# A four-layer graph network: edge masks gathered in another layer, first blocks prepared before the table, four gather buffers, dense tiles kept off the end of the list, two row-end steps a tile

## Chip, cores and metric

The kernel runs on one core of a Trainium2 chip. The metric is the device time of one execution in microseconds. Before the change it is 3169.53 us, the median of three executions (3165.16 to 3173.18).

## What is computed

Four attention layers over one graph of N = 4096 nodes with C = 256 features. `adj` is a 4096 x 4096 matrix of 0 and 1 in int32; an edge is likelier among the low-numbered nodes, so the first rows have many edges and the last few. Every layer is followed by a residual sum and a LayerNorm. In short:

```
h = x @ W                                    # per layer
logit[i, j] = leaky_relu(f1[i] + f2[j])      # layer 0: 8 heads, + gate * sum_f Wc[f] * |curv[i,f] - curv[j,f]|
logit = where(adj > 0, logit, -big)          # layer 1: one head, no leaky_relu; layer 2: 4 heads
att = softmax(logit, over j);  out = att @ h # layer 2: elu(out) + x @ Wr + br, norm
x = layernorm(x + out)                       # layer 3: three such layers with elu (3.1, 3.2, 3.3), then the norm
```

## The kernel before

**Sparse work.** A tile has P = 128 partitions. Where the rows of a chunk or pair of chunks have few edges, the kernel does not go over all 4096 columns: it makes a list of the columns that have an edge, and fetches their rows of a table in HBM by an indirect DMA, which GpSimd issues. One such DMA fetches 128 rows and is called a gather here.

**Layer 0** (`layer0`, L770) goes by the 32 row chunks of 128 rows. Chunk 0 is dense (`rows0`, L448, all 32 column tiles, spread over the others by `next(dense)`). Chunks 1 to 31 go by their edges (`rows_by_edges`, L600): `EDGE_TILES[c]` tiles of 128 edges, 445 in all, in blocks of up to ten. A block has these steps:

- `middle` and `spread` (L626, L632) find which row every edge belongs to (VectorE, ScalarE and TensorE), and `nodes` (L641) makes from this the indices `idx` of the edges' nodes;
- `gather` (L656) fetches the rows of `table0`, one indirect DMA per tile (L659), into a buffer `g` of the pool `l0_got`, which has three;
- `differences`, `pair_terms`, `weights`, `values` (L662 to L689) make the attention weights and multiply the fetched rows by them. The first to read a gather is `d` (L666);
- `rows` and `add` (L691, L699) sum the rows by matmuls with a 0/1 matrix (L702). These matmuls are the last to read `g`, and free its buffer.

The loop at the end of the function calls these steps for blocks i to i + 4. The gather of block i + 2 is issued right after `values` of block i. The instructions of each engine run in the order that the tile scheduler has given them, which the source order and its own estimates decide; a queue does not overtake.

**Lists and masks.** Beside the blocks, `lane` (L1193) gives every tile a share of other work: `list_edges` (finds the columns of the next chunks' edges, almost all of it on VectorE, L905 to L922), `list_pairs` (the lists of columns for the pairs of chunks that the later layers use) and `job`. A pair q is 256 rows; of the 16 pairs, pair q has `PAIR_TILES[q]` tiles of 128 listed columns: 32, 25, 22, 20, 19, 18, 17, 16, 16, 15, 15, 14, 14, 14, 13, 13. For each listed tile of pairs 1 to 15 (251 tiles) a mask of 128 x 256 is needed. `listed_mask` (L1017) fetches it from the adjacency by an indirect DMA on GpSimd (L1020), converts it to bytes on VectorE (L1024), and SyncE writes it to `listed_d` in HBM. `LATE = 13` says which pairs' masks are made in layer 0: pairs 1 to 12, 211 tiles. The masks of pairs 13 to 15 (40 tiles) are put into `late_jobs` and made in layer 1 by `late_masks` (L1417). `mask_bytes` (L392, conversion at L402) makes byte masks for the pairs that are done densely. The job queue lets 7 masks be under way.

**Start of layer 0.** The first projection runs over 32 tiles; after every fourth, six steps of `list_edges` are taken. Then VectorE scales the 32 tiles of `V` (L1175), and SyncE writes each to `table0` (L1177). Only then does `rows_by_edges` open its pools, in memory that `V` and its neighbours have used, and make its constants: `number`, `place`, `count` (L707 to L712) and two memsets each for `dTs` (L619).

**Layers 1 to 3** go by pairs of chunks. `sequence` (L1252) sets the order of the tiles: the first `LEAD` dense tiles (`DENSE` says how many pairs are dense: 6 in layer 1, 1 in layer 2, 3 in each part of layer 3), then the listed tiles in order of the pairs, with the remaining dense tiles spread evenly among them. `attend` (L1266) runs over this order: for each tile the weights (VectorE, ScalarE) and, two tiles later, the products (TensorE: L1414, L1515 and L1519, L1605). After each tile it takes one step of `aside` and `rate` steps of the row ends, which norm the finished rows and project them for the next layer (L198, L209, L213). `rate` is 1.0 by default, 1.6 in layer 2. The gathers of these layers are at L1312. After the last tile the projection's sums set the next layer's scale, `V` is scaled, and the next table is written.

Of the kernel before, what the change touches and what calls it, by code (L numbers as in the profile page):

```python
# [54 lines left out]
I32 = mybir.dt.int32  # L55
# [19 lines left out]

LATE = 13
# [4 lines left out]
def gnn_stack(ctx: ExitStack, tc: tile.TileContext, a: dict, out: bass.AP):  # L81
# [366 lines left out]
    def rows0(chunks, ends, ps, ps_s, ps_acc):  # L448
# [3 lines left out]
        with ExitStack() as st:  # L452
            two = st.enter_context(tc.tile_pool(name="l0_all_two", bufs=2))
            three = st.enter_context(tc.tile_pool(name="l0_all_three", bufs=2))
            got = st.enter_context(tc.tile_pool(name="l0_all_got", bufs=3 * JR))
# [144 lines left out]
    def rows_by_edges(prepared, pair_w, ends, ps, lane, first):  # L600
# [8 lines left out]
        with ExitStack() as st:  # L609
            two = st.enter_context(tc.tile_pool(name="l0_two", bufs=2))  # L610
            got = st.enter_context(tc.tile_pool(name="l0_got", bufs=3))
            ps_acc = st.enter_context(tc.tile_pool(name="l0_acc", bufs=2, space=PSUM))
            ps_x = st.enter_context(tc.tile_pool(name="l0_x", bufs=2, space=PSUM))
            number = two.tile([P, BT, P], U16, name="number", bufs=1)
            place = two.tile([P, max(EDGE_TILES)], F32, name="place", bufs=1)
            count = two.tile([P, P], F32, name="count", bufs=1)
            dTs = [two.tile([ROW1 + 1, P], F32, name=f"dT{k}", bufs=1) for k in range(2)]
            for d in dTs:
                nc.vector.memset(d[0:ROW1], 0.0)  # L619
                nc.vector.memset(d[ROW1:], 1.0)  # L620
# [83 lines left out]


            number_i = two.tile([P, BT * P], I32, name="number_i", tag="to_row")
            nc.gpsimd.iota(number_i, pattern=[[1, BT * P]], base=0, channel_multiplier=0)  # L707
            nc.vector.tensor_copy(number.rearrange("p t r -> p (t r)"), number_i)
            nc.vector.tensor_copy(count, number_i[:, 1:P + 1])
            place_i = two.tile([P, max(EDGE_TILES)], I32, name="place_i", bufs=1)  # L710
            nc.gpsimd.iota(place_i, pattern=[[P, max(EDGE_TILES)]], base=1, channel_multiplier=1)
            nc.vector.tensor_copy(place, place_i)  # L712

# [6 lines left out]
            def at(i, *what):  # L720
                if 0 <= i < B:
                    for w in what:
                        getattr(plan[i], w)()

            dense = first(lambda shape, name: ps_x.tile(shape, F32, name=name, tag="x"),
                          lambda shape, name: ps_acc.tile(shape, F32, name=name, tag="acc0", bufs=1))
            given = 0
            for i in range(3):
                at(i, "middle", "spread", "nodes")
# [1015 lines left out]
```

## Time and profile before

| what | value |
|---|---|
| median of three executions | 3169.53 us |
| the profiled execution | 3159.55 us, its span 3157.8 us |
| TensorE busy | 2574.0 us, 82% of the span |
| VectorE busy | 2277.2 us, 72% |
| ScalarE busy | 1329.2 us, 42% |
| GpSimd busy | 1966.0 us, 62% |
| mean granted TensorE clock | 0.881 |
| gathers of layer 0 (L659) | 445, mean 1158 ns |
| gathers of masks (L1020) | 251, mean 1112 ns |
| gathers of layers 1 to 3 (L1312) | 1010, mean 1102 ns |

The stages, as the timeline shows them: layer 0 from 0 to about 1205 us (first gather 135.27, last 1149.66), layer 1 to about 1487, layer 2 to 2225, layer 3.1 to 2538, 3.2 to 2850, 3.3 to the end.

The page gives the span in 40 equal slices, one row per engine, a digit being the busy share in tenths; the row PEclk is the clock granted to TensorE, in tenths of full speed. The windows give for stretches of the span the busy time and, in brackets, the number of instructions of PE (TensorE matmuls), PEld (weight loads), DVE (VectorE), ACT (ScalarE) and POOL (GpSimd), then the granted clock, the busy share of the DMA engines and their GB/s. A row of groups reads: line, engine, operation, what it writes and reads, shapes, count, busy time and mean ns of one, and after the second bar the time that the engine stood idle just before these instructions, with what ended it: "<-DMA g<-table,idx 54.2" means that 54.2 us ended with the landing of a gather, "issue" that nothing shown was waited for. A row of the timeline reads: start, duration, engine, line, operation, what it writes and reads, count.

### The profile page before, as it was taken

Reading aid. Unit: us, or ns where it says so; the run is one execution under the profiler, and the core shown is the slowest. Engines: PE = TensorE matmul, PEld = TensorE weight load, DVE = VectorE, ACT = ScalarE, POOL = GpSimd, SP = SyncE. Lnnn points to the kernel's source line nnn. Section 1 sums busy time; section 2 is a strip of 40 time slices with the busy share of each in tenths; the row PEclk is TensorE's granted clock in tenths of the full one; section 3 lists DMA queues with packets and bytes.
Section 4 is the critical chain, followed back from the end, with each engine's and each line's share of the span. In section 5 each row is a group of like instructions: output and inputs, shape, how many; then the busy total and the mean of one; then the engine's idle time right before and its main releaser. Section 6 shows DMA issues by size and latency. Waiting matters only on the chain.

```text
span 3157.8 us, 53737 instructions
## 1 busy us (share of the span) xinstructions
PE 2574.0 (82%) x16067; PEld 1798.6 (57%) x16067; DVE 2277.2 (72%) x7545; ACT 1329.2 (42%) x3895; POOL 1966.0 (62%) x1874
## 2 busy tenths in 40 slices
PE   6266666656666556998999999998899999999997
PEld 5154454444545445996233333333788878887875
DVE  6767888888888856776878788886565556556666
ACT  3365565646666434776212223333222322233334
POOL 0277667777777756772475566551477647755775
PEclk8587777777676778998999999999999999999999
DMA  6567786657666447675333333331544454446554
GB/s 183 164 195 224 234 249 190 206 169 220 198 217 204 115 128 233 200 206 155 105 89 101 96 104 99 100 86 51 171 137 135 114 174 135 135 113 183 166 164 129
DMA packets 345937, 495.65 MB, mean 157 GB/s; under 512 B 120476, under 2 KB 252418, under 8 KB 345634
## 3 DMA queue, kind: packets, MB, share of 16 engines
q0 software_dynamic: 87600, 252.16, 28.5%
q1 hardware_dynamic: 239608, 223.19, 23.6%
q10 hardware_dynamic: 18432, 16.79, 1.6%
q8 instruction: 132, 2.16, 0.3%
q14 instruction: 165, 1.35, 0.1%
HBM read 426.20 MB, written 65.72 MB: 156 GB/s over the span
## 4 chain that ended last, share of the span: by engine, by line
PE 51%; DMA 4%; DVE 2%; ACT 2%; issue 1%; POOL 0%; ACTq 0%; DVEq 0%; SPq 0%; POOLq 0%
PE acc L1605 20%; PE num L1515 12%; PE den L1519 8%; PE acc L1414 4%; PE ph L209 4%; DMA g<-table,pair_idx 3%; PE xT_p L198 1%; PE pr L213 1%; DVE w L1599 1%; PE pt L1537 0%; ACT V L1585 0%; POOL g L1312 0%; DVE y L1617 0%; DVE bn_st L305 0%; DVE y L314 0%
## 5 line engine op out<-in xcount | busy, mean ns | idle before, releaser
L1312 POOL DMA_INDIRECT g<-table,pair_idx x1010 | 1113.5, 1102 | 523.4 <-PE den L1519 102.6
L659 POOL DMA_INDIRECT g<-table,idx x445 | 515.5, 1158 | 194.0 <-issue 116.5
L1605 PE MATMUL acc<-g,w 128*128 128x257 f32 x2448 | 574.7, 382 | 17.3 <-DVE w L1599 16.7
L1605 PEld LDWEIGHTS acc<-g,w 128*128 128x128 f32 x2448 | 457.9, 190 | 94.7 <-DVE w L1599 30.0
L1506 DVE SCALAR_TENSOR_TENSOR w<-R,g,mask 128x256 f32<-128x256 f32 x1004 | 438.4, 486 | 48.2 <-PE den L1519 47.9
L1599 DVE SCALAR_TENSOR_TENSOR w<-R,g,mask 128x256 f32<-128x256 f32 x612 | 292.2, 482 | 244.8 <-PE acc L1605 172.8
L1515 PE MATMUL num<-w,g 128*64 128x256 f32 x2008 | 367.6, 395 | 0.0
L1020 POOL DMA_INDIRECT pair_m<-in_adjT,cell x251 | 279.2, 1112 | 112.4 <-issue 46.0
L702 PE MATMUL acc<-g,to_row 128*128 128x264 f32 x890 | 304.4, 502 | 41.3 <-DVE g L689 32.5
L1605 PE MATMUL acc<-V,w 128*128 128x257 f32 x1152 | 284.6, 387 | 16.1 <-ACT V L1585 9.1
L702 PEld LDWEIGHTS acc<-g,to_row 128*128 128x128 f32 x890 | 216.1, 255 | 95.1 <-DVE g L689 38.7
L1519 PE MATMUL den<-w,g 128*1 128x256 f32 x2008 | 266.5, 378 | 0.0
L1515 PEld LDWEIGHTS num<-w,g 128*64 128x64 f32 x2008 | 140.5, 135 | 196.9 <-DVE w L1506 97.4
L1605 PEld LDWEIGHTS acc<-V,w 128*128 128x128 f32 x1152 | 221.4, 194 | 49.7 <-ACT V L1585 15.0
L1615 ACT ACTIVATE y<-acc,inverse 128x256 f32<-128x256 f32 x96 | 44.7, 466 | 417.2 <-DVE inverse L320 365.9
L209 PE MATMUL ph<-wx,xT 128*128 128x258 f32 (+3 forms) x640 | 185.4, 423 | 33.4 <-ACT xT L200 19.7
L1599 DVE SCALAR_TENSOR_TENSOR w<-R,V,mask 128x256 f32<-128x256 f32 x288 | 137.0, 481 | 87.0 <-PE acc L1605 74.2
L905 DVE FIND_INDEX8 cand<-ones,near 128x8 uint16<-128x520 bf16 (+8 forms) x424 | 195.1, 469 | 0.0
L696 ACT ACTIVATE to_row<-count,side 128x128 f32<-128x128 f32 x445 | 145.4, 391 | 102.8 <-PE acc L702 99.5
L200 ACT ACTIVATE xT<-xT_p 128x128 f32<-128x128 f32 x320 | 86.0, 276 | 196.3 <-PE xT_p L198 187.2
L874 ACT ACTIVATE near<-ai 128x64 bf16<-128x64 int32 (+1 forms) x186 | 138.4, 765 | 59.4 <-DMA ai<-in_adj 31.2
L209 PEld LDWEIGHTS ph<-wx,xT 128*128 128x128 f32 x640 | 125.7, 206 | 64.8 <-ACT xT L200 31.4
(327 smaller groups left out, 4290.2 us busy)
## 6 DMA issues: line engine op xcount, KB each, us to landing
ai<-in_adj SPq DMA_DIRECT2D x124, 512.0 KB
mask<-listed_d SPq DMA_DIRECT2D x228, 128.0 KB
at<-in_adjT SPq DMA_DIRECT2D x96, 256.0 KB
mask<-mask_d SPq DMA_DIRECT2D x128, 128.0 KB
g<-table,pair_idx POOLq DMA_INDIRECT x1010
R<-r_d SPq DMA_DIRECT2D x56, 256.0 KB
table<-V POOLq DMA_DIRECT2D x12, 1032.0 KB
s<-y ACTq DMA_DIRECT2D x96, 128.0 KB
```

Source lines behind the costliest of these rows:

```text
L209: nc.tensor.matmul(ph, xT[:, kt, :], self.wx[:, kt, :], start=kt == 0, stop=kt == 1)
L659: nc.gpsimd.indirect_dma_start(self.g[:, t, :], None, table0[:, :], bass.IndirectOffsetOnAxis(ap=self.idx[:, t:t + 1], axis=0))
L696: nc.scalar.activation(self.to_row[:, t], count, AF.Abs, bias=self.side[:, t, 0:1])
L702: nc.tensor.matmul(acc, self.to_row[:, t], self.g[:, t, 0:VW], start=self.t0 + t == 0, stop=last and t == n - 1)
L905: nc.vector.max_index(cand[:, s], ones8, near[:, at:at + W])
L1020: nc.gpsimd.indirect_dma_start(m[:, :], None, pair_cells, bass.IndirectOffsetOnAxis(ap=cell[:, k:k + 1], axis=0))
L1312: nc.gpsimd.indirect_dma_start(g[:, :], None, self.table[:, :], bass.IndirectOffsetOnAxis(ap=pair_idx[:, at:at + 1], axis=0))
L1506: nc.vector.scalar_tensor_tensor(w[:, h], R[:, h].rearrange("p t i -> p (t i)"), g[:, VW2 + h:VW2 + h + 1], m, ALU.max, ALU.mult)
L1515: nc.tensor.matmul(num[h % 2 * D2:(h % 2 + 1) * D2, h // 2, :], g[:, h * (D2 + 1):h * (D2 + 1) + D2], w[:, h], start=False, stop=last and ...
L1519: nc.tensor.matmul(den[32 * h:32 * h + 1, :], g[:, (h + 1) * (D2 + 1) - 1:(h + 1) * (D2 + 1)], w[:, h], start=False, stop=last)
L1599: nc.vector.scalar_tensor_tensor(w, R[:, q * PW:(q + 1) * PW], g[:, C + 1:C + 2], m, ALU.max, ALU.mult)
L1605: nc.tensor.matmul(t, w[:, it * P:(it + 1) * P], g[:, 0:C + 1], start=k == 0, stop=last)
```

## The change

It has seven parts.

1. `LATE` goes. Masks of pairs 6 to 15 (147 tiles) are made in layer 0; those of pairs 1 to 5 (104 tiles), which layer 1 does densely, are made in layer 2: `late_masks` moves from `layer1` to `layer2`, where listed pairs now go 6 to 15 and then 1 to 5.
2. The pools of `rows0` are opened in `layer0` ahead of `rows_by_edges`, so that the pools of the blocks no longer lie in the memory of `V`. The constants `number`, `place`, `columns` (before: `count`) and `dTs` are made at the start of layer 0. Thereby the first blocks' index work may run beside the table's write.
3. `l0_got` has four buffers instead of three; the gather of block i + 3 is issued with its `nodes`, where the gather of block i + 2 was issued after `values` of block i.
4. The first projection takes four steps of `list_edges` after every fourth tile instead of six: 32 instead of 48.
5. Every fourth tile of `V` is scaled on GpSimd instead of VectorE (8 of 32), and the table is written by 8 DMAs of four tiles instead of 32.
6. `SPARE = 24`: the remaining dense tiles are spread over all but the last 24 listed ones.
7. `rate` is 2.0 in all of layers 1 to 3.

```diff
-LATE = 13
-    def rows0(chunks, ends, ps, ps_s, ps_acc):
+    def rows0(chunks, ends, ps, ps_s, ps_acc, st):
...
-            got = st.enter_context(tc.tile_pool(name="l0_got", bufs=3))
+            got = st.enter_context(tc.tile_pool(name="l0_got", bufs=4))
...
-            number = two.tile([P, BT, P], U16, name="number", bufs=1)
-            place = two.tile([P, max(EDGE_TILES)], F32, name="place", bufs=1)
-            count = two.tile([P, P], F32, name="count", bufs=1)
-            dTs = [two.tile([ROW1 + 1, P], F32, name=f"dT{k}", bufs=1) for k in range(2)]
...
+            number, place, count, dTs = consts
...
             for i in range(3):
-                at(i, "middle", "spread", "nodes")
-                if i < 2:
-                    at(i, "gather")
+                at(i, "middle", "spread", "nodes", "gather")
...
                 blk.values()
-                at(i + 2, "gather")
                 at(i + 1, "pair_terms")
                 lane(share, c)
-                at(i + 3, "nodes")
+                at(i + 3, "nodes", "gather")
...
+            number = lp.tile([P, BT, P], U16, name="number")
+            place = lp.tile([P, max(EDGE_TILES)], F32, name="place")
+            columns = lp.tile([P, P], F32, name="columns")
...
+                now = q >= DENSE[1]
...
-                if q < LATE:
+                if now:
                     jobs.extend([lambda i=i: listed_mask(at_pool, q, i, cell) for i in range(A)])
...
                     if T % 4 == 3:
-                        for _ in range(6):
+                        for _ in range(4):
                             next(edge_lists)
...
                     for T in range(NT):
-                        nc.vector.tensor_tensor(by_head[:, T], by_head[:, T],
-                                                v[:, T, :].unsqueeze(2).to_broadcast([P, H0, D0 + 1]), ALU.mult)
-                        nc.sync.dma_start(table0[T * P:(T + 1) * P, :], V[:, T, :])
+                        (nc.gpsimd if T % 4 == 3 else nc.vector).tensor_tensor(
+                            by_head[:, T], by_head[:, T], v[:, T, :].unsqueeze(2).to_broadcast([P, H0, D0 + 1]), ALU.mult)
+                        if T % 4 == 3:
+                            nc.sync.dma_start(table0[(T - 3) * P:(T + 1) * P, :].rearrange("(t p) c -> p t c", p=P), V[:, T - 3:T + 1, :])
...
+    SPARE = 24
...
+        among = max(len(later) - SPARE, 1)
...
-            while given * len(later) < len(rest) * (n + 1) and given < len(rest):
+            while given * among < len(rest) * (n + 1) and given < len(rest):
...
-    def attend(seq, opened, weights, products, ends, rate=1.0, batch=1, lag=2, aside=iter(())):
+    def attend(seq, opened, weights, products, ends, rate=2.0, batch=1, lag=2, aside=iter(())):
...
-            attend(seq, opened, weights, products, lambda ended: ends_of(ended, NP, nxt, ps, one), aside=late_masks())
+            attend(seq, opened, weights, products, lambda ended: ends_of(ended, NP, nxt, ps, one))
...
-            attend(seq, opened, weights, products, lambda ended: ends_of(ended, NP, nxt, ps, one), rate=1.6, batch=2)
+            attend(seq, opened, weights, products, lambda ended: ends_of(ended, NP, nxt, ps, one), batch=2, aside=late_masks())
...
+            listed = list(range(k, NP))
+            if n == 2:
+
+                listed = [q for q in listed if q >= DENSE[1]] + [q for q in listed if q < DENSE[1]]
+            return sequence(range(k), listed, LEAD[n])
```

In the order of instructions that the scheduler gives the changed kernel, GpSimd issues 278 gathers of layer 0 before the first mask, then 167 gathers mixed with 147 masks; none in layer 1; 31 masks before layer 2's table is written, and 73 among its first gathers.

## Prediction

> **What bounds the kernel now.** I read the shares in slices first, then the stretches of layer 0, then who waits in them. Page, part 2:
>
> ```profile
> PE   6266666656666556998999999998899999999997
> DVE  6767888888888856776878788886565556556666
> POOL 0277667777777756772475566551477647755775
> PEclk8587777777676778998999999999999999999999
> ```
>
> Each digit is a fortieth, 79 us. TensorE is full from digit 17 on, at a granted clock of 0.9 and more: layers 1 to 3. Digits 1 to 16 are layer 0: TensorE at 0.6, VectorE at 0.8, GpSimd at 0.7, none full on average. What a change in layer 0 is worth must come from its stretches. The windows, cut at the first gather (135.27 us), at gathers 81, 181 (near 501) and 278 of 445 (263, 505, 747), and at the last (1149.66):
>
> ```profile
> core 0: us, PE busy (x) PEld busy (x) DVE busy (x) ACT busy (x) POOL busy (x), PEclk, DMA share, GB/s
> 0.00:135.00 135.00, 62.35 (x376) 50.84 (x376) 104.13 (x500) 47.16 (x147) 8.32 (x109) 0.72 0.60 174
> 135.00:263.00 128.00, 85.89 (x653) 66.91 (x653) 87.83 (x255) 74.68 (x213) 92.92 (x80) 0.79 0.68 199
> 263.00:505.00 242.00, 153.97 (x1150) 117.95 (x1150) 195.97 (x733) 140.24 (x371) 162.59 (x145) 0.74 0.79 236
> 505.00:747.00 242.00, 147.55 (x1176) 112.56 (x1175) 196.69 (x782) 140.11 (x373) 190.77 (x168) 0.72 0.64 192
> 747.00:950.00 203.00, 129.82 (x1077) 98.58 (x1077) 178.75 (x743) 124.91 (x334) 151.84 (x136) 0.71 0.67 204
> 950.00:1076.00 126.00, 75.77 (x645) 59.47 (x642) 108.43 (x431) 67.03 (x172) 99.76 (x86) 0.69 0.58 172
> 1076.00:1150.00 74.00, 47.10 (x328) 36.48 (x328) 51.54 (x150) 38.58 (x112) 57.58 (x45) 0.79 0.45 127
> ```
>
> GpSimd from 505 to 747: 168 indirect DMAs (97 gathers, 71 masks) are 190.77 us busy; the timeline puts 0.30 us between one and the next, 50 us; together 241 of 242. There its queue is the bound, at 242/168 = 1.44 us each. From 747 to 1076 it is 222 in 329, 1.48 each: nearly so. From 135 to 263 it makes 80 in 128 us, and nothing is full. Who waits there, for VectorE and GpSimd, 135 to 747:
>
> ```profile
> L1024 DVE TENSOR_SCALAR pair_mb<-pair_m 128x256 uint8<-128x256 int32 x110 | 32.8, 304 | 30.5 <-DMA pair_m<-in_adjT,cell 15.7 <-issue 10.1 <-DMA listed_d<-pair_mb 4.7
> L666 DVE TENSOR_TENSOR d<-g,side 128x42 f32<-128x42 f32 (+4 forms) x40 | 7.9, 198 | 67.0 <-DMA g<-table,idx 54.2 <-DMA pair_m<-in_adjT,cell 6.1 <-issue 4.3
> ```
> ```profile
> L659 POOL DMA_INDIRECT g<-table,idx x277 | 314.9, 1137 | 135.8 <-issue 72.8 <-PE acc L702 32.3 <-PE s L508 12.7
> ```
>
> VectorE is busy 87.83 + 195.97 + 196.69 = 480 of these 612 us, idle 132: of that 67.0 at `d`, the first reader of a gather, and 30.5 at the conversion of a mask. The gathers themselves stood 32.3 us for a product of TensorE (L702), which frees their buffer: one of three. So the first half runs on VectorE's work plus waits for late gathers.
>
> **Part 1: masks (L977, L1011, L1417).** Layer 0 loses pairs 1 to 5 (104 gathers at L1020) and gains pairs 13 to 15 (40); layer 1 loses those 40; layer 2 gains 104. The order of the changed kernel puts no mask before gather 278, then 167 gathers with 147 masks.
> First half: VectorE's 480 us lose 33 (110 conversions at 304 ns). Their 30.5 us of idle go too.
> Second half: 314 indirect DMAs instead of some 264. I take 1.47 us each (between 1.44 and 1.48): 462 us, where 747 to 1150 took 403. VectorE has 339 + 15 us of work there, under 80%, so GpSimd is the bound. Bounds: 1.44 (452 us) and the dearest stretch, 1076 to 1150, 74 us for 44 gathers, 1.68 (528 us).
> Tail of layer 0 (1150 to 1205, 55 us) holds 21 masks and their conversions in VectorE's queue between the last rows; I take 48. If other work fills it: 55.
> Start of layer 1, 1205 to 1250: TensorE is busy 32.24 of 45 us, its products wait 15.4 us, 11.0 of it for ScalarE's pieces. Masks still stand in three queues there. I take half, −7; 0 if only the pieces count, −15 if all goes.
> Into layer 2: 31 masks stand ahead of the table's first write on GpSimd. They may start when layer 1's mask buffers fall free, about 1452; 31 by 1.25 us (spacing of the masks from 1174 on) end at 1491, where that write was issued at 1489.80. On VectorE 22 conversions precede the first weights: 1452 + 22 by 1.25 + 3 for the last landing = 1482, against a first product at 1487.69. I take +4, with −5 (two row tiles fewer at the end of layer 1) and +10 as ends.
> Within layer 2: TensorE is busy 262.31 of 263 us from 1487 on, VectorE 215.39; the 73 masks spread there add 73 by 0.30 = 22, so 90%. VectorE stays hidden, but closer. GpSimd: a gather and 0.7 masks at 1.28 us (its pace where layer 3 fills it) are 2.2 us, against TensorE's 2.4 a tile. I take +6; 0 if all is covered, +32 (104 by 0.304) if VectorE becomes the bound.
>
> **Parts 2 to 4: start of layer 0.** VectorE is nearly full from 50 to 105 (47.4 of 50 us in the slice 50 to 100). 16 of 48 list steps move behind the first gather; a step is 54 us of list work / 48 = 1.1 us. Of 18 us I take 15; none if the loads of the adjacency rows set the pace. The 18 come back in the first half.
> Scaling the table starts at 104.6 and takes 11.1 us, and the first gather follows 19.6 us after its end: until 126.6 the constants (L707) and VectorE's memsets wait for the old table's memory, and only then come the first blocks' indices. In the changed order, 29 list operations (7.7 us at the place where they stood, 115.6 to 123.3) and some 6 us of index work follow the scaling at once; the table's last write lands beside this. Eight of 32 tiles go to GpSimd, whose nearest row is an addition of 128x256:
>
> ```profile
> 1866.19 1.00 POOL L1527 TENSOR_TENSOR xr<-xr,beta 128x256 f32<-128x256 f32 x1
> ```
> ```profile
> 1864.90 2.96 DVE L1506 SCALAR_TENSOR_TENSOR w<-R,g,mask 128x256 f32<-128x256 f32 x5
> 1868.32 0.87 DVE L1506 SCALAR_TENSOR_TENSOR w<-R,g,mask 128x256 f32<-128x256 f32 x2
> ```
>
> Two undisturbed weights take 0.87, so five should take 2.07; beside the addition they take 2.96, 0.89 more. I take that for each of the eight: 24 by 0.335 + 8 by 0.89 = 15.1 us, 4 more than now; without it, 3 less.
> The Trainium skill, SBUF — State Buffer, section Who interferes with whom, says that a VectorE instruction with two inputs in SBUF and a GpSimd instruction that reads SBUF exclude each other for a whole instruction. It speaks against this part, and the row agrees; without the rule and the row, the first gather would come 7 us earlier.
> First gather: 104.6 − 15 + 15.1 + 7.7 + 6 = 118, against 135.3.
>
> **Part 3: fourth gather buffer.** A gather is issued a block ahead of where it was, behind an older product. I take half of the 67.0 us of idle at `d` away, 33; the ends are 0 and 67. It also puts gather 278 a block (some 5 to 7 tiles at 1.9 us) ahead of the arithmetic: −10.
>
> **Sum for layer 0.** First half: work 480 − 33 + 18 = 465, idle 132 − 30.5 − 33 = 69: 534 us. Then 118 + 534 − 10 + 462 + 48 = 1152, against 1205: −53. Check: gathers alone would need 278 by 1.44 = 400, so GpSimd is not the bound in the first half; TensorE's 387 busy us are not either.
>
> **Parts 6 and 7: dense tiles, row ends.** Layers 3.1 and 3.2 (2225 to 2520: TensorE 294.42 of 295) keep their work; the row end of pair 15 may stand barer. Layer 3.3 ends in a chain of gathers; two row tiles left at the end instead of four. I take +3; ends −5 and +6.
>
> **Total:** −53 − 7 + 4 + 6 + 3 = −47. The profiled execution took 3159.55 us (span 3157.8), 10 us under the median of 3169.53. So 3112.5 on its own scale, 3122 on the median's.
>
> **Rivals** (on the median's scale; measurement can tell 0.3%, 9.5 us, from no change).
> A. The fourth buffer brings nothing: `d` waits 67 us as now. For it: a gather still stands behind indices that VectorE makes late in its own queue. Against it: 32.3 us of the gathers' idle were for a buffer. +34: **3156**, faster by 0.4%.
> B. Slower: the second half of layer 0. 314 indirect DMAs pass in one order, and each gather stands behind up to 11 masks, whose conversions wait for landings. Its price is us per DMA. The sum breaks even at 1.47 + 47/314 = 1.62. At 1.68, the pace of 1076 to 1150, it is 528 us: +66, **3188**. For it: 1.67 in 263 to 505 (242/145) too. Against it: there buffers or indices held GpSimd; with 71 masks to 97 gathers it ran at 1.44.
> C. The idle at `d` goes wholly (−33) and the second half runs at 1.44 (−9): **3080**. For it: nothing else held 135 to 263, with every engine under 73%.
> D. Masks do not hide in layer 2: VectorE, 90% by my sum, becomes the bound. +26: **3148**.
>
> **Numbers.** Forecast 0.46, A 0.18, B 0.13, C 0.12, D 0.11. The forecast and C are faster; A 0.12 faster, 0.05 within, 0.01 slower; D 0.08, 0.02, 0.01; B slower. Faster 0.78, same 0.07, slower 0.15. The range reaches from C with the scaling at its cheaper end (3080 − 7 = 3073) to B at 1.65 us (314 by 0.18 = 57: 3179): 3072 to 3178.
>
> **What would show it.** First gather near 118; gather 278 near 642 with no mask before it; then no idle of GpSimd beyond 0.30 us, and the last gather near 1104; idle at `d` before gather 278 some 34 us; layer 1 with no gap at its start; layer 2's TensorE still full, VectorE near 90% in its first 260 us. I am wrong if VectorE keeps 100 us of idle in the first half, if an indirect DMA costs over 1.6 us in the second, or if layer 2 is longer by 20 us.

## The result and the profile after

The changed kernel takes 3167.18 us, the median of four executions (3159.98 to 3168.98); the kernel before took 3167.35 us beside it. The ratio is 0.9994, with a 95% interval from 0.9971 to 1.0017: no change. The prediction was 3122 (3072 to 3178), faster with a chance of 0.78. That 3167 lies inside the stated range is luck: the range reached up there for the price of rival B, and that price did not come. The profiled execution took 3166.24 us, its span is 3164.4, against 3157.8 before. The rows of the page's second part that answer to those shown of before:

```profile
PE   6367767766675448997999999997999999998996
DVE  6768899889887536777787888886565555556765
POOL 1376566467777724776677766751577557755775
```

VectorE is fuller in the first ten slices (digits 8 and 9), and GpSimd is mostly less busy in slices 4 to 9, where masks had stood. So the work was moved as planned, and the end did not come sooner. From the first product of one layer to the first of the next, in us of the two traces:

| stage | before | after | predicted change | found |
|---|---|---|---|---|
| layer 0, to the first product of layer 1 | 1205.5 | 1185.5 | -53 | -20.0 |
| layer 1, to the first product of layer 2 | 282.2 | 290.6 | -3 (-7 + 4) | +8.4 |
| layer 2 | 737.2 | 743.8 | +6 | +6.6 |
| 3.1, 3.2, 3.3 | 313.3, 312.2, 307.5 | 319.3, 317.7, 307.6 | +3 together | +6.0, +5.5, +0.1 |

Twenty microseconds are won in layer 0, where 53 were forecast, and twenty-seven are given back later. Layer 0 first. Its stretches after the change, cut at gathers 1, 81, 181 and 278 (columns as before):

```profile
119.00:251.00 132.00, 86.78 (x624) 66.16 (x625) 82.62 (x262) 74.10 (x216) 87.06 (x80) 0.79 0.68 200
251.00:467.00 216.00, 145.74 (x1115) 107.95 (x1113) 184.41 (x715) 134.65 (x361) 124.52 (x102) 0.78 0.79 235
467.00:670.00 203.00, 149.78 (x1242) 113.13 (x1243) 186.71 (x722) 142.84 (x383) 115.26 (x98) 0.79 0.55 170
```

Without masks GpSimd is busy 115 of 203 us, VectorE 187: in the last of these stretches VectorE is the bound (92%). But the first is as it was: 80 gathers in 132 us, VectorE 63%. The groups of VectorE and of GpSimd from 119 to 670, after:

```profile
L661 DVE TENSOR_TENSOR d<-g,side 128x42 f32<-128x42 f32 (+4 forms) x40 | 7.9, 198 | 49.5 <-DMA g<-table,idx 49.4
```
```profile
L654 POOL DMA_INDIRECT g<-table,idx x278 | 327.5, 1178 | 244.7 <-issue 118.8 <-PE acc L697 94.4 <-DVE of_row L630 20.8
```

The idle at `d` (L666 before, L661 now) went from 67.0 to 49.5 us. The gathers wait for a buffer longer than before, 94.4 us against 32.3, though there is one buffer more: with no masks in GpSimd's queue they come to its head early and stand there.

Then layer 2's start, GpSimd's timeline after the change:

```profile
1480.31 34.15 POOL L1023 DMA_INDIRECT pair_m<-in_adjT,cell  x1 [0.30 <-DMA pair_m<-in_adjT,cell]
1514.76 1.06 POOL L1023 DMA_INDIRECT pair_m<-in_adjT,cell  x1 [0.30 <-DVE w L1503]
1515.83 3.63 POOL L1486 DMA_DIRECT2D table<-V  x4
1533.33 1.20 POOL L1320 DMA_INDIRECT g<-table,pair_idx  x1 [13.88 <-issue]
```

One mask, the 30th of 31 ahead of the table, holds GpSimd for 34.15 us, and the next instruction starts only at 1514.76. Layer 2's first product stands 11.6 us earlier than before the change, its first gather 14.3 later (1533.3 against 1519.0). VectorE beside it:

```profile
1475.53 39.87 DVE L1503 SCALAR_TENSOR_TENSOR w<-R,V,mask 128x256 f32<-128x256 f32 x100 [0.70 <-DMA R<-r_d]
```

And in the tail of layer 3.1 TensorE does the row ends that are left. First before the change, after its last product at 2519.6, then after the change, with the last product at 2519.9:

```profile
2521.05 1.14 PE L209 MATMUL ph<-wx,xT 128*128 128x258 f32 x4 [0.91 <-ACT xT L200]
```
```profile
2522.59 0.69 PE L196 MATMUL xT_p<-ident,y 128*128 128x128 f32 x2 [2.71 <-DVE y L312]
2523.74 2.09 PE L207 MATMUL ph<-wx,xT 128*128 128x258 f32 x4 [0.46 <-ACT xT L198]
```

Four row tiles were left before, two now. But the two wait 2.71 us for VectorE's `y`, and four matmuls then take 2.09 us instead of 1.14. The next stage's sums (L239, now L237) start 8.3 us after the last product before, and 8.7 after. The row ends moved into the full stretch of products (3.1: 300.0 us from its first product to its last, before 294.7), and the tail behind it got no shorter. TensorE has no room in that stretch, before and after (columns of the windows):

```profile
2225.00:2520.00 295.00, 294.42 (x1370) 255.73 (x1370) 175.28 (x451) 70.29 (x270) 204.67 (x206) 0.99 0.50 142
2220.00:2520.00 300.00, 299.89 (x1380) 253.12 (x1380) 177.40 (x453) 69.45 (x287) 205.01 (x207) 0.99 0.50 140
```

### The profile page after: what moved, and what is told of

It is laid out like the page before. It is cut to its first block, busy times and chain, and to the rows that moved or that the text cites. A ratio compares the mean times of both kernels' runs of the same rounds, so it can differ in the third digit from the quotient of the medians.

```text
span 3164.4 us, 53679 instructions
## 1 busy us (share of the span) xinstructions
PE 2608.1 (82%) x16067; PEld 1796.8 (57%) x16067; DVE 2282.2 (72%) x7537; ACT 1324.5 (42%) x3897; POOL 1995.7 (63%) x1882
## 4 chain that ended last, share of the span: by engine, by line
PE 43%; DMA 3%; DVE 2%; issue 2%; ACT 1%; POOL 1%; DVEq 0%; ACTq 0%; SPq 0%; POOLq 0%
PE acc L1613 22%; PE num L1512 10%; PE den L1516 7%; PE ph L207 3%; DMA g<-table,pair_idx 2%; PE xT_p L196 1%; POOL g L1320 1%; PE pt L1545 0%; ACT V L1593 0%; DVE w L1503 0%; DVE w L1607 0%; DMA pair_m<-in_adjT,cell 0%; DVE bn_st L303 0%; ACT L310 0%; DVE y L312 0%
## 5 line engine op out<-in xcount | busy, mean ns | idle before, releaser
L1320 POOL DMA_INDIRECT g<-table,pair_idx x1010 | 1096.2, 1085 | 449.6 <-issue 89.2
L654 POOL DMA_INDIRECT g<-table,idx x445 | 526.9, 1184 | 298.6 <-issue 165.0
L1023 POOL DMA_INDIRECT pair_m<-in_adjT,cell x251 | 307.6, 1225 | 81.9 <-issue 30.2
L697 PE MATMUL acc<-g,to_row 128*128 128x264 f32 x890 | 311.8, 511 | 41.2 <-DVE g L684 32.1
L1516 PE MATMUL den<-w,g 128*1 128x256 f32 x2008 | 273.7, 378 | 0.0
L1613 PEld LDWEIGHTS acc<-V,w 128*128 128x128 f32 x1152 | 220.8, 193 | 47.4 <-ACT V L1593 13.7
L207 PE MATMUL ph<-wx,xT 128*128 128x258 f32 (+3 forms) x640 | 193.7, 435 | 39.8 <-DVE p_f L218 21.3
L691 ACT ACTIVATE to_row<-columns,side 128x128 f32<-128x128 f32 x445 | 146.6, 391 | 114.9 <-PE acc L697 110.2
L1027 DVE TENSOR_SCALAR pair_mb<-pair_m 128x256 uint8<-128x256 int32 x251 | 76.9, 308 | 111.9 <-DMA pair_m<-in_adjT,cell 67.9
```

The lines of the kernel that those rows point to most:

```text
L207: nc.tensor.matmul(ph, xT[:, kt, :], self.wx[:, kt, :], start=kt == 0, stop=kt == 1)
L654: nc.gpsimd.indirect_dma_start(self.g[:, t, :], None, table0[:, :], bass.IndirectOffsetOnAxis(ap=self.idx[:, t:t + 1], axis=0))
L691: nc.scalar.activation(self.to_row[:, t], count, AF.Abs, bias=self.side[:, t, 0:1])
L697: nc.tensor.matmul(acc, self.to_row[:, t], self.g[:, t, 0:VW], start=self.t0 + t == 0, stop=last and t == n - 1)
L1023: nc.gpsimd.indirect_dma_start(m[:, :], None, pair_cells, bass.IndirectOffsetOnAxis(ap=cell[:, k:k + 1], axis=0))
L1320: nc.gpsimd.indirect_dma_start(g[:, :], None, self.table[:, :], bass.IndirectOffsetOnAxis(ap=pair_idx[:, at:at + 1], axis=0))
```

## The experiments

The theory to test (G): each part acts in its own stage; part 1 wins in layer 0 and pays in layer 2, and parts 6 and 7 give back what was won. The main rival (H): the later layers are longer for what part 1 put into them or took out. The ratios are to the kernel before on the same chip, with 95% intervals.

**Part 7 undone.**

```diff
-    def attend(..., rate=2.0, ...)
+    def attend(..., rate=1.0, ...)      # and rate=1.6 in layer 2
```

> The changed kernel with part 7 undone: one row-end step a tile in layers 1 and 3, 1.6 in layer 2. In the changed kernel layer 0 ends 15 to 20 us earlier, but layer 1's products then last 257 us instead of 250, and those of 3.1 and 3.2 300 instead of 294. Theory G (given back by parts 6 and 7): earlier row ends put their matmuls into the stretch of products, where TensorE is full, and the tail after the last product does not get shorter, because it is a chain through VectorE and ScalarE and not TensorE's work. Then layer 1 returns to 250 to 252, 3.1 and 3.2 lose 2 to 5 us each, and the time falls by 8 to 14 us from the changed kernel's 3167. Rival H (the layers are longer because of what part 1 put into or took out of them, or because their state at the start differs): the three stretches stay within 2 us, and the time within 4 us.

Measured: 0.9933 (0.9912 to 0.9955), 3151.15 us. Layer 1 takes 282.4 us as before the change, 3.1 and 3.2 312.6 and 312.2: all given back, 8.2 + 6.7 + 5.5 us. Layer 2, though, takes 753.8 instead of 743.8: there two steps help. That is theory G for part 7, with sizes somewhat above those expected (2 to 5 us in 3.1 and 3.2, 8 to 14 in all).

**Part 6 undone.**

```diff
-    SPARE = 24
+    SPARE = 0
```

> The changed kernel with part 6 undone: dense tiles spread to the end of the list (SPARE = 0). Theory G: the last 24 tiles of the list have no dense work beside them, so at the end of layer 1 products wait for the pieces of the gathered rows (3 us idle in its last 58), and the rest of the listed tiles is only moved. Undoing it gives 2 to 4 us in layer 1 and 0 to 3 in each of 3.1 and 3.2: 3 to 9 us less than the changed kernel. Rival H: no stretch moves by more than 1 us, the time stays within 3 us.

Measured: 0.9958 (0.9939 to 0.9977), 3156.55 us. Layer 1 stays at 290.9 us: its products last 6.9 us less (250.5 instead of 257.4), as theory G has it, and the way from its last product to layer 2's first is 7.2 us longer (40.4 instead of 33.2), with four row tiles left to do there (in the changed kernel two and the last matmuls of a third). 3.1 and 3.2 are 316.5 and 317.3, which is 2.8 and 0.4 less; most of the gain is in layer 2, 735.5 instead of 743.8, though part 6 does not touch its order (all 32 dense tiles are its lead). No mask was caught there this time. So G is not confirmed for part 6; its own worth lies under 3 us in a stage, and the interval overlaps the changed kernel's.

**Masks held back until V is scaled.**

```diff
+    zero = lp.tile([P, A], I32, name=f"zero{q}")
+    nc.vector.tensor_scalar(zero, V[:, NT - 1, 0:A], 0.0, None, ALU.mult)
+    moved[q] = lp.tile([P, A], I32, name=f"moved{q}")
+    nc.vector.tensor_tensor(moved[q], cell, zero, ALU.add)
```

> The changed kernel, but the late masks of layer 2 take their indices from a copy that waits for the last scaled tile of V, so that they can't be issued ahead of the table's write. In the changed kernel the 30th of the 31 masks issued ahead of that write took 34.15 us, inside an unbroken row of 84 weights on VectorE, and the table was written 14 to 26 us later than in the kernel before. Theory S (a mask caught in the row of weights holds the table): the table's writes follow ScalarE's scaling again, the first gather comes near 1510 instead of 1533, TensorE's 5.6 us of idle in the first 100 us of layer 2 go, and the time falls by 4 to 8 us. Rival T (the hold only goes over to the next indirect DMA, or the lead of 32 dense tiles covers it): the first gather of layer 2 or the first mask takes over 20 us instead, and the time stays within 3 us.

Measured: 1.0000 (0.9986 to 1.0014). No indirect DMA of layer 2's first 100 us takes over 5 us, and the first gather comes at 1517.3 instead of 1533.3: theory S for the hold. But nothing is won. VectorE in layer 2, this kernel, then the changed one:

```profile
L1031 DVE TENSOR_SCALAR pair_mb<-pair_m 128x256 uint8<-128x256 int32 x104 | 30.3, 292 | 61.8 <-issue 41.0 <-DMA pair_m<-in_adjT,moved 12.9 <-DVE w L1507 7.6
```
```profile
L1027 DVE TENSOR_SCALAR pair_mb<-pair_m 128x256 uint8<-128x256 int32 x82 | 25.2, 308 | 50.7 <-issue 22.4 <-DMA pair_m<-in_adjT,cell 21.5 <-DVE w L1503 3.0
```

The masks now stand behind the table in GpSimd's queue, and VectorE's queue stands 61.8 us at their conversions, with the weights behind them. Layer 2's first product comes 8.0 us earlier than in the changed kernel (1468.1 against 1476.1), and its products last 10 us longer (721.3 instead of 711.2). A wait was exchanged for another: the time is rival T's, the reason neither's.

**Parts 2 to 5 alone** (parts 1, 6, 7 undone).

> The kernel before with parts 2 to 5 only: early constants and blocks beside the table, four buffers, fewer list steps in the prologue, the table in 8 writes; masks, dense tiles and row ends as before. If layer 0's gain comes from the start and the buffers (theory P), the first gather is at 119, the first half is slower than the changed kernel's for its 114 masks, the second faster, the last gather comes at 1125 to 1135, and with nothing given back later the time is 3167 - 20 = 3147. If moving the masks carries it (theory M), the last gather comes at 1140 or later, GpSimd being full with masks and gathers, and the time is within 8 us of the kernel before.

Measured: slower, 1.0100 (1.0080 to 1.0119), 3203.18 us. The first gather comes at 121.4, but gather 278 at 765.0 and the last at 1186.2, later than before the change. VectorE's idle before gather 278 is 170 us instead of 132: 59.0 at `d`, 42.3 at conversions. Neither theory had it slower. A gather of part 3 stood 38.2 us at the head of GpSimd's queue for a buffer, with masks behind it.

**Part 3 undone.**

```diff
-    got = st.enter_context(tc.tile_pool(name="l0_got", bufs=4))
+    got = st.enter_context(tc.tile_pool(name="l0_got", bufs=3))
...
                 blk.values()
+                at(i + 2, "gather")
...
-                at(i + 3, "nodes", "gather")
+                at(i + 3, "nodes")
```

> The changed kernel with part 3 undone: three gather buffers, gather of block i + 2 after the values of block i. The prediction put 33 us of saved idle at d and 10 us of lead down to part 3. Theory B (the fourth buffer does carry the first half): idle at d before gather 278 rises from 49 us to 65 to 80, gather 278 comes at 685 to 700 instead of 670, the time is 10 to 25 us above the changed kernel's. Theory C (part 3 is worth nothing, since gathers now only stand longer for a buffer, 96 us at the products, and hold up what is behind them): gather 278 stays within 8 us of 670, the second half gets no longer, and the time is within 6 us of the changed kernel's or under it.

Measured: 0.9967 (0.9953 to 0.9981), 3155.76 us, under the changed kernel. Gather 278 is at 675.9 (6 us later), the last product of layer 0 at 1151.6 (7 us earlier). And the idle at `d`, from 118 to 676:

```profile
L661 DVE TENSOR_TENSOR d<-g,side 128x42 f32<-128x42 f32 (+4 forms) x40 | 7.7, 193 | 46.7 <-DMA g<-table,idx 46.6
```

It is no more than with four buffers (49.5). That is theory C; the time itself is not clear of the changed kernel's, since the two intervals overlap.

**Parts 6 and 7 undone together.**

> The changed kernel with parts 6 and 7 both undone. Each alone gave 0.7 and 0.4%. If they act apart (theory G), the ratio to the kernel before is 0.988 to 0.991, about 3137 us, layer 1 lasting 248 us and 3.1 and 3.2 294 each. If both gave back the same microseconds (rival), it is 0.993, about 3150.

Measured: 0.9959 (0.9944 to 0.9973), 3155.52 us. Layers 1 and 3 are as theory G has them (layer 1 281.8, 3.1 311.6), but layer 2 takes 750.2, with a mask caught for 35.3 us, and the ratio lies above what both theories gave. In the medians the single gains do not add up. In the profiled executions they nearly do: the span is 16.6 us under the changed kernel's, with part 7 undone 7.4, with part 6 undone 11.0, of which 8.3 are layer 2 without a caught mask.

**Parts 2, 4 and 5 alone** (as parts 2 to 5, with three buffers).

> The kernel with parts 2 to 5, slower by 1% than the one before, with part 3 undone as well: early constants, lighter prologue and table in 8 writes alone. Theory C (with the masks of pairs 1 to 12 in layer 0, the gathers of part 3 stand at the head of GpSimd's queue for a buffer, once for 38 us, and hold the masks behind them, for which VectorE then waits 42 + 20 us): without part 3 the last gather comes at 1135 to 1145 instead of 1186, and the time is 3150 to 3162. Rival L (the 16 list steps put off, and the table, cost it): the last gather stays above 1170 and the time above 3185.

Measured: 1.0085 (1.0067 to 1.0104), 3194.15 us; last gather at 1179.0. Theory C fails here: part 3 is not what makes these parts slow when 211 masks stay in layer 0. From gather 121 to 161 it needs 113 us where the kernel before needs 88; it issues nine masks there, the kernel before none, and VectorE is idle 16.7 us at the conversion of `at` and 10.6 at `d`, where it was 5.5 and 3.4. The granted clock is 0.68 there, before 0.79. Which part does it was not tried.

**Part 1 alone.**

```diff
-                if q < LATE:
+                if q >= DENSE[1]:
```

with `late_masks` in layer 2 and its order, all else as before.

> The kernel before with part 1 alone: masks of pairs 1 to 5 in layer 2. If moving the masks is worth what the prediction's first half said (33 us of conversions and 30 of idle for 52 more in the second half), the last gather comes 5 to 20 us before 1150, layer 1 keeps its 250 us and starts up to 7 us sooner, layer 2 is 8 to 17 us longer for waits at conversions: 3150 to 3170. If it needs parts 2 to 5 beside it to pay (the parts enable each other), the time is 3170 or more, and the changed kernel's gain in layer 0 is neither the one's nor the other's.

Measured: 0.9937 (0.9915 to 0.9958), 3149.82 us. The last gather comes at 1135.6, layer 1 starts at 1182.7 (the changed kernel: 1185.5), its products last 242.4 us instead of 250.3, layer 2 takes 745.9 instead of 737.2. In this profile no mask was caught, and VectorE's conversions stand 0.5 us in layer 2, yet its products last 714.6 us instead of 703.4. From layer 1's last product to layer 2's first it is 41.4 us instead of 31.9. So part 1 alone wins all that the changed kernel wins in layer 0. The idle at `d` with part 1 alone, 138 to 681:

```profile
L666 DVE TENSOR_TENSOR d<-g,side 128x42 f32<-128x42 f32 (+4 forms) x40 | 7.8, 195 | 39.0 <-DMA g<-table,idx 38.2 <-issue 0.6
```

Three buffers, late first blocks, and 39.0: it is the masks leaving the first half that brought the gathers forward. The stretches say the same. Idle at `d` in us, with the masks issued there in brackets:

| kernel | gathers 1 to 81 | 81 to 181 | 181 to 278 |
|---|---|---|---|
| before | 33.7 (0) | 23.1 (41) | 10.2 (73) |
| part 1 alone | 33.5 (0) | 5.4 (0) | 0.1 (10) |
| changed kernel | 42.4 (0) | 7.1 (0) | 0.1 (0) |

The idle went where the masks had been, and half of it stood where there never was one. Whether the masks held the gathers in GpSimd's queue, or their conversions held the gathers' indices in VectorE's, no run separates; that GpSimd's queue was full is shown for the last stretch alone (241 of 242 us).

**Part 1 with two row-end steps in layer 2 only.**

```diff
-            attend(..., rate=1.6, batch=2, aside=late_masks())
+            attend(..., rate=2.0, batch=2, aside=late_masks())
```

> The kernel before with part 1, and of part 7 only layer 2's share: two row-end steps a tile there, one in layers 1 and 3. In the runs with part 1, layer 2's products last 703 to 711 us at two steps and 715 to 721 at 1.6. Theory G (earlier row ends help layer 2, whose TensorE follows VectorE, and hurt layers 1 and 3): layer 2's products last 703 to 709 us against 714.6 with part 1 alone, all other stretches as there; the time is 3138 to 3145, ratio near 0.991. Rival: layer 2's length goes by where a mask is caught, not by the rate; it stays at 711 or more and the time at 3147 to 3153.

Measured: 0.9871 (0.9846 to 0.9896), 3133.09 us, 1.3% under the kernel before. Layer 2's products last 702.9 us, against 714.6 with part 1 alone, and in neither profile was a mask caught: theory G for layer 2's length. That TensorE follows VectorE there is not shown: both profiles have TensorE busy through layer 2's products. First part 1 alone, then with two steps (columns as in the windows above):

```profile
1466.50:2181.60 715.10, 715.08 (x4824) 250.76 (x4824) 584.33 (x1632) 196.80 (x597) 460.67 (x358) 1.00 0.40 111
1460.90:2164.40 703.50, 703.48 (x4824) 247.66 (x4824) 583.31 (x1632) 197.64 (x598) 455.62 (x359) 1.00 0.41 113
```

**The same, masks converted seven later.**

```diff
-                    if len(begun) > 4:
+                    if len(begun) > 7:
```

> As the run with part 1 and two row-end steps in layer 2, but a late mask is converted seven masks after its gather was issued, not four. Theory V (in layer 2 VectorE's queue stands at conversions whose mask has not landed, 36 to 62 us in the runs with masks there, and the weights behind them come late to TensorE): the idle at the conversions falls under 15 us, layer 2 is 3 to 8 us shorter than with four, the time 3 to 8 us less. Rival: that idle is covered, TensorE being full; layer 2 stays within 2 us.

Measured: 0.9888 (0.9863 to 0.9914). Idle at the conversions in layer 2 is 5.4 us, but it was 3.4 already with four. The test had nothing to take away, and says nothing on theory V. Layer 2's products last 707.8 us, 4.9 more, which neither expectation had.

**A break in the row of weights** (changed kernel).

```diff
+                if not nodes.listed:
+                    pause = work.tile([1, 1], F32, name="pause", bufs=2)
+                    nc.vector.tensor_copy(pause, w[0:1, 0, 0:1])
```

> The changed kernel, with one copy of a single element on VectorE after the four weights of each dense tile in layer 2, a break in the row of weights. Theory S (an indirect DMA that is caught while VectorE runs scalar_tensor_tensor back to back gets no further until the first break; the mask of 34.15 us ended 0.73 us after a gap of 89 ns in a row of 84 weights): no indirect DMA in the first 60 us of layer 2 takes over 4 us, the table's first write comes at 1485 to 1495 instead of 1515.8, the first gather near 1510; the time moves by 6 us at most, since the 32 dense tiles cover it. Rival Q (the mask stood for its buffer, its landing or a full queue): it takes 20 us or more again.

GpSimd's timeline there, and VectorE's:

```profile
1480.42 1.27 POOL L1023 DMA_INDIRECT pair_m<-in_adjT,cell  x1 [0.30 <-DVE w L1503]
1482.00 1.34 POOL L1023 DMA_INDIRECT pair_m<-in_adjT,cell  x1 [0.31 <-DVE w L1503]
1483.33 0.96 POOL L1486 DMA_DIRECT2D table<-V  x1
...
1506.34 1.74 POOL L1320 DMA_INDIRECT g<-table,pair_idx  x1 [5.12 <-issue]
```
```profile
1480.86 1.65 DVE L1503 SCALAR_TENSOR_TENSOR w<-R,V,mask 128x256 f32<-128x256 f32 x4
1482.44 0.13 DVE L1507 COPY pause<-w 1x1 f32<-1x1 f32 x1
```

The same masks take 1.27 and 1.34 us, the table follows ScalarE again, the first gather is 27 us earlier, and the idle at the conversions in layer 2 falls from 50.7 to 8.3 us. Layer 2's products last 705.4 us instead of 711.2, and the time is 3159.39, 0.9955 (0.9936 to 0.9974). So theory S holds and rival Q does not: the break takes the hold away. This is one profile, but the twelve kernels that have masks ahead of the table and no break all show a hold of over 10 us in this row (last section). The price in the trace, 5.8 us of layer 2's products, is what was expected; that the median lies lower still is not shown, since its interval overlaps the changed kernel's.

**Part 4 undone** (in parts 1 to 5).

```diff
-                        for _ in range(4):
+                        for _ in range(6):
                             next(edge_lists)
```

> Parts 1 to 5 with part 4 undone: six list steps after every fourth tile of the first projection. Theory L (the lighter prologue is a loan: 16 list steps are VectorE's work of 18 us, which layer 0 does either way, and it ends by VectorE's work and waits): the first gather comes at 128 to 137 instead of 118, the last product of layer 0 at 1148 to 1158 as with four steps (1153.6), the time within 5 us of 3155. Rival: the earlier start is kept, and giving it up costs 10 to 18 us: last product 1164 to 1172, the time 3166 to 3174.

Measured: 0.9912 (0.9890 to 0.9934), 3146.76 us. First gather at 133.3, last product of layer 0 at 1152.8, with four steps 118.4 and 1153.6: a loan, theory L. But its time did not come: it is 9 us less than with four, and the intervals do not meet (0.9934 against 0.9944). No mask was caught in this profile, and its span is that of the profile with four (3148.2 and 3147.8 us), so where the medians part is not shown.

Since the parts had been timed in different company, three more runs add them one by one to the kernel with part 1 and layer 2's two steps.

> The kernel with part 1 and layer 2's two row-end steps (ratio 0.987 to the kernel before), with parts 2 and 5 added: constants made early, first blocks' indices beside the table, table scaled on two engines and written in 8 DMAs. Theory K (this is the one saving at the start that is no loan: the chain from the scaling to the first gather gets shorter): first gather at 128 to 134 instead of 138, last product of layer 0 3 to 8 us earlier than the 1148 to 1154 without, ratio 0.984 to 0.987. Rival (layer 0 ends by VectorE's work and waits, so an earlier first gather brings nothing): last product at 1148 to 1156, ratio 0.987 to 0.990.

> As the run with parts 1, 2 and 5, with part 4 added: four list steps instead of six. Theory L (loan): first gather 10 to 15 us earlier, near 118, last product of layer 0 within 4 us of the run without part 4, ratio within 0.002 of it. Rival: the earlier start is kept, and the ratio falls by 0.003 to 0.005.

> As the run with parts 1, 2, 4 and 5, with part 3 added: the fourth gather buffer and the earlier gather. Theory C (worth nothing or less: with the masks gone from the first half, idle at d falls to 39 to 47 us with three buffers already; the block of lead leaves more to do after the last gather): idle at d before gather 278 within 5 us, the span from the last gather to the last product 5 to 12 us longer, last product no earlier, ratio equal or up to 0.003 higher. Rival B (the prediction's: 33 us of idle and 10 of lead): last product 15 or more earlier, ratio lower by 0.005 or more.

| kernel (part 1, layer 2 at two steps) | first gather | gather 278 | last product of layer 0 | ratio |
|---|---|---|---|---|
| and no more | 139.4 | 678.5 | 1148.3 | 0.9871 (0.9846 to 0.9896) |
| + 2, 5 | 135.2 | 676.4 | 1145.0 | 0.9878 (0.9862 to 0.9895) |
| + 2, 5, 4 | 116.1 | 670.1 | 1143.9 | 0.9875 (0.9857 to 0.9892) |
| + 2, 5, 4, 3 | 119.8 | 662.2 | 1150.4 | 0.9889 (0.9872 to 0.9906) |

Parts 2 and 5 bring 4 us at the first gather and 3 at the last product. Part 4 brings 19 at the first gather and 1 at the end. Part 3 puts gather 278 8 us ahead and the last product 6.5 back. Theory K has its last product, but the ratio is its rival's; theories L and C hold. In time, none of the four differs from another, though a mask was caught in the last two profiles (for 36.1 and 34.5 us) and not in the first two. The 36.1 us cost layer 2's products 4 to 5 us (707.8 instead of 702.9 and 703.6). The idle at `d` before and with part 3:

```profile
L661 DVE TENSOR_TENSOR d<-g,side 128x42 f32<-128x42 f32 (+4 forms) x40 | 7.7, 192 | 47.6 <-DMA g<-table,idx 47.5
```
```profile
L661 DVE TENSOR_TENSOR d<-g,side 128x42 f32<-128x42 f32 (+4 forms) x40 | 7.8, 196 | 45.2 <-DMA g<-table,idx 45.1
```

## Why the prediction was wrong, step by step

**The sum for layer 0** was 118 + 524 + 462 + 48 = 1152; it came as 119.3 + 550.4 + 457.7 + 58.1 = 1185.5.

- First gather: right (119.3 against 118), by errors that cancel. The scaling starts 11.7 us earlier and not 15 (92.97 instead of 104.6); it takes 11.3 us and not 15.1; from its end to the first gather it is 15.0 us and not 13.7. The price of scaling on two engines was too high. Its rows, before, then after on VectorE and on GpSimd:

```profile
104.62 11.08 DVE L1175 TENSOR_TENSOR V<-V,v 128x264 f32<-128x264 f32 x32
```
```profile
93.50 10.80 DVE L1178 TENSOR_TENSOR V<-V,v 128x264 f32<-128x264 f32 x23
```
```profile
92.47 6.05 POOL L1178 TENSOR_TENSOR V<-V,v 128x264 f32<-128x264 f32 x8 [81.90 <-ACT v L1175]
```

  While GpSimd scales its tiles, VectorE's come 0.77 us apart instead of 0.34, so each of GpSimd's cost VectorE 0.43 us, where 0.89 was taken from an addition of nearly the same size. For 24 tiles instead of 32 VectorE needs as long as before. That the list steps would come back was in the sum.
- Second half: right. 308 indirect DMAs took 457.7 us, 1.49 each, with the bound on GpSimd (it stood idle 97.6 us there, 0.32 us a DMA, little over the 0.30 between any two), where rival B needed 1.62.
- First half: the failed step, 550.4 us instead of 524. The prediction took 33 us of idle at `d` and 10 of lead from the fourth buffer. The idle did fall, from 67.0 to 49.5 us, but it is 39.0 with part 1 alone and 46.7 without part 3: the masks had kept some of the gathers back, and the buffer had not. The row "<-PE acc L702 32.3" said what the gathers waited for, not that anyone waited for the gathers on its account. Rival A said that the fourth buffer brings nothing, and was given 0.18; the 67 us that it left at `d` did not stay either, since part 1 took some away, and its 3156 had nothing for what parts 6 and 7 cost. The sum had 34 us left at `d`, so 15.5 too few. Beside it the idle at `mb` (a byte mask's conversion) rose from 12.2 to 18.6 us and at `last` (a step of `list_edges`) from 3.9 to 10.1, terms that the sum left as they were, against 11 us less work than summed.
- The lead: gather 278 did come earlier for part 3, and the end did not. After the last gather the changed kernel needs 31.5 us to its last product, before 24.3, with three buffers 22.9. GpSimd's place is no measure of the layer's end when the arithmetic is behind it. This is most of the 10 us in the tail (58.1 instead of 48).

**Start of layer 1** (-7): right. The products of layer 1 last 7.9 us less with part 1 alone (242.4 instead of 250.3). In the changed kernel they last 257.4: undoing part 7 takes 8.8 away, undoing part 6 takes 6.9.

**Into layer 2** (+4, ends -5 and +10): with part 1 alone it is +9.5 (41.4 us from layer 1's last product to layer 2's first, before 31.9), the upper end. In the changed kernel it is +1.3: with parts 6 and 7 together fewer row tiles are left there, and layer 1's products are longer for it.

**Layer 2** (+6): the size was right (+6.6) by luck, since it is the sum of three terms that the prediction did not have. By the lengths of its products: part 1 without a caught mask makes them 11.2 us longer (703.4 to 714.6). A caught mask adds 8.2 (711.2 in the changed kernel, 703.0 without part 6, where none was caught). Two row-end steps take 11.7 away (702.9 instead of 714.6). VectorE did not become the bound: it is busy 209 of the first 263 us, 80% and not 90, and TensorE is full, at 200 of 200 us from 1776. Why part 1 costs 11 us with TensorE full and no mask caught, by the masks or by the new order of the pairs, no run separates.

**Parts 6 and 7** (+3, ends -5 and +6): the other failed step. I looked at layer 3 alone and took two row tiles fewer at the end as a gain. Part 7's row ends cost 8.2 us in layer 1, 6.7 in 3.1 and 5.5 in 3.2: they stand where TensorE is full (299.89 of 300 us in 3.1), and the tail, where it waits for VectorE's `y` and ScalarE's `xT`, was not shorter. The two tiles that moved are not the whole of it: without part 6 four are left as before, and 3.1's products still last 297.7 us against 294.7. What the rest is, no run separates.

**Rivals B, C and D**: B's price did not come; C's idle did not go; D's bound did not come, and layer 2 lost 6.6 us instead of 32.

What stays open: why parts 2, 4 and 5 cost 0.85% when the masks stay in layer 0; what part 6 is worth alone, some 3 us in the traces and nothing clear of noise in the times; and what holds the first 80 gathers, which take 127 to 140 us in all seventeen kernels, with no mask among them and no engine full in the two windows shown.

## What to carry to other kernels

Where one engine waits for another's result, ask what stands ahead of that result in its queue before adding buffers: 28 of the 67 us of idle here went when other work, 1.4 us a piece in GpSimd's queue, was moved away, and a fourth buffer took away at most 2.4. Work that is put off from a prologue into a stage bound by the same engine is a loan, and an earlier start is worth only what the end shows. The same rate of row ends shortened one layer and lengthened three (layer 2's products 11.7 us less; layers 1, 3.1 and 3.2 8.2, 6.7 and 5.5 more), so a rate belongs to a layer and not to the kernel: part 1 with two steps in layer 2 alone runs at 0.987.

## What the runs showed of the hardware

An indirect DMA on GpSimd can stand beside an unbroken row of VectorE instructions that read several operands in SBUF, not for one instruction but for dozens. The mask of 34.15 us stood beside 84 `scalar_tensor_tensor` of 0.48 us; the first gap, of 89 ns, came 0.73 us before its end, and another gather of 10.33 us ended 0.73 us after a gap of 90 ns. Masks of the same row just before had taken 0.95 to 1.22 us, so not each is caught. Of the fourteen kernels with masks in layer 2, six show one such hold of a mask in their profiled execution, of 32.6 to 36.1 us. In six more the masks were through in time, and the first gather of layer 2 was held instead, for 10.5 to 13.1 us; all six ended 0.88 us or so after the row's first gap began. The last two are the kernel with its masks behind the table, and the one with a copy of a single element after every four weights of the dense tiles: there no indirect DMA of layer 2's first 100 us took over 5 us. Among its listed tiles, which have no such copy, gathers of 6 to 12 us remain.

That the gap is what ends a hold is shown only in part. Of the six held masks four ended 0.82 us after the first gap began. The other two (32.6 and 34.5 us) ended some 0.8 us ahead of the next gap, with the row still unbroken.

The Trainium skill, SBUF — State Buffer, section Who interferes with whom, says that a VectorE instruction with two inputs in SBUF contends with a GpSimd instruction that reads SBUF, that the shared ports are an exclusive lock, and (of VectorE's two-port modes) that whoever issues first has them for the whole instruction and the other is blocked. The direction agrees, the length does not: 34.15 us is the row's, not an instruction's 0.48, and here the measurement decides. The next instruction's start at 1514.76 says the same as the duration.
